# Folding a weight product into an earlier stage of a graph attention kernel, and moving a scaling to ScalarE

## The chip, the cores and the metric

The kernel runs on one core of a Trainium2 chip. The metric is the device time of one execution in microseconds (us). Before the change the median of three runs is 673.04 us (671.46 to 673.52).

## The reference

Two layers run over 4096 nodes of 512 features, with an adjacency matrix of 4096 x 4096 integers in which one entry in about a thousand is set (some four neighbours a node).

```
Wh   = x @ W[h]                                # 8 heads of 64
e    = leaky_relu(f1[i] + f2[j], 0.2)          # f1, f2 = Wh @ a[h] (two halves)
out  = softmax(where(adj > 0, e, -9e15)) @ Wh  # heads side by side
x    = layernorm(x + out)
agg  = (adj > 0) @ x / max(degree, 1)
out  = relu(concat(x @ W_self + b_self, agg @ W_nb + b_nb) @ W_comb + b_comb)
x    = layernorm(x + out)
```

The second layer has no nonlinearity between its two products, so that x @ (W_self W_c1) and agg @ (W_nb W_c2) do, with W_c1 and W_c2 the halves of W_comb. The kernel makes these two 512 x 512 products on the chip; in the code they are m1 (W_self) and m2 (W_nb), and the biases go the same way into one row, brow.

## The kernel before, in words

The nodes are 32 blocks of 128 rows, and the adjacency is used as a list of neighbours a node. The work has three stages. The order of the instructions is written out by hand; each engine carries out its own in that order and waits on semaphores where data or a buffer is missing.

**The lists** (loop over b, from line 929). SP's queue loads x (line 338, 256 KB a block) and adj (line 413, two tiles of 1 MB a block, four buffers named at). ScalarE turns each tile into a mask (mask_adj, line 419), which frees the adj buffer. PE transposes x (line 346; ScalarE copies the result, lines 352 and 359), multiplies it with the weights of the first layer (node_half, line 367; VectorE copies, line 371), and packs the masks into keys (fold_adj, line 437). VectorE takes the largest keys (line 452). Every four blocks a decode (line 454) makes lists, indices and owner tables out of the keys; it is a generator, and each call of some(lists) runs one piece of it, most of them short VectorE work. POOL stores the rows into the table t0 (line 926).

**The joint** (lines 955 to 1013). m2's weights wr and wc are loaded on SP's queue behind adj of block 30, ahead of that of block 31. fold_weights(loaded, place2, "pw") then makes m2 in 16 steps. For each of four chunks, PE transposes a slice of the weights (turned, line 293), ScalarE copies it (line 294), PE does four matmuls (line 305, two instructions each), one a step, and ScalarE copies the sum back into the weights' own tile (line 309). The steps stand between the last masks and folds of blocks 30 and 31. The first two gathers of table rows stand there too; the buffer of the second lies where the adj tiles were, so it waits for the last mask.

**The attention stage** (loop over i from -3 to 33, line 1021). One turn has several blocks in work at different depths. For each block POOL gathers five table rows a node (line 612: three of the node's own list, two from a list that the block shares). VectorE adds and weighs them (lines 645, 662, 670, 686). PE adds the shared rows (a_shared, line 696). VectorE takes the reciprocal of the softmax sum (line 704). The eight heads are then scaled: six on ScalarE, one instruction each (line 712), and two in one VectorE instruction (line 715). VectorE adds x (line 722), ScalarE normalises (root and norm, lines 730 to 739). PE multiplies with m2 to get z (line 744), ScalarE copies it (line 748) and SP stores it in t1 (line 749). PE transposes the block, ScalarE copies it (line 352), and SP stores it in xt (line 752). Five gather buffers stand for the rows. Each turn from i = -2 on also runs one piece of the remaining decodes, and from i = 17 on the pieces of late_lists (line 550). From i = 28 on POOL gathers z rows for the last stage: gather_early(b) reads t1 up to block 25 + b, so it waits until those z are stored.

At i = 7 SP loads W_self into m1 and W_c1 into wc; at i = 16 to 19 VectorE adds the self bias (line 324), and at i = 20 sum_bias (line 329) makes the bias row.

**The last stage** (from line 1072). For each block PE adds the shared z rows (g_shared, line 783) and x @ m1 (g_self, line 776), onto a bias row that ScalarE has copied (line 767). VectorE adds gathered rows (lines 761 and 763) and scales and clips (lines 799 and 803); ScalarE normalises; SP stores. POOL gathers five z rows a node and block, with seven buffers. Between the first two blocks' shared sums and the first x @ m1 stands the fold of W_self, all 16 steps:

```
    for _ in fold_weights(loaded, place, "key"):
        pass
```

Of the kernel before, what the change touches and what calls it, by code (L numbers as in the profile page):

```python
# [31 lines left out]
F32 = mybir.dt.float32  # L32
# [80 lines left out]
def listed_layers(  # L113
# [34 lines left out]
    FIRST = (0, 1, 3)  # L148
    EARLY = NB - 3
    LB = NB - 2  # L150
    HA = 6
# [145 lines left out]
    def fold_weights(loaded, place, bank):  # L297

        wr, wc = loaded
        wT = turned(wr, 0, place(0), bank)  # L300
        for c in range(FB):
            nxt = turned(wr, c + 1, place(c + 1), bank) if c + 1 < FB else None
            mp = ps.tile([P, HD], F32, name="mp")
            for d in range(FB):
                nc.tensor.matmul(  # L305
                    mp, lhsT=wT[:, d, :], rhs=wc[:, d, :], start=(d == 0), stop=(d == FB - 1)
                )
# [398 lines left out]
    def a_scale(b):  # L706

        for h in range(HA):
            a, q = divmod(h, H // 2)
            o = a * HD + (1 - a) * H + q * D  # L710
            s = NM[b][:, o : o + D]
            nc.scalar.mul(s, s, RD[b][:, h : h + 1])  # L712
        o = HD + HH - (H - HA) * D
        s = NM[b][:, o : HD + HH].rearrange("p (h d) -> p h d", d=D)
        nc.vector.tensor_tensor(
            s, s, RD[b][:, HA:].unsqueeze(2).to_broadcast([P, H - HA, D]), OP.mult
        )
# [98 lines left out]
    def some(todo):  # L816
        for p in todo:
            next(p, None)
# [105 lines left out]

    def store(w, row, eng=nc.scalar):
        eng.dma_start(t0[2 + w * P : 2 + (w + 1) * P, :], row[:, 0:TW])

    w, lists = 0, []
    for b in range(LB - 1):
        for k in range(1 + (b in AHEAD)):  # L930
            load_x(w + k + XL)
        load_adj(b + 2, ap)
        if b == 4:
            pads(wp)
# [12 lines left out]
        for k in range(2):  # L947
            some(lists)
        if b == 25:
            pieces = mean_row(w_sb, sums, xa)  # L950
# [4 lines left out]
    m2 = weight(fp, "wr")  # L955
    loaded = load_fold(1, w_nb, m2, weight(fc, "wc"))
# [3 lines left out]
    mask_adj(LB, 0)  # L960
# [6 lines left out]
    def place(c):  # L967
        return wp.tile([P, FW], F32, name="row", bufs=2)[:, 0:FIN]

    def place2(c):  # L970
        return last.rearrange("p (a g) k -> p a (g k)", a=2)[:, c % 2, :]

    def pieces(n, todo):
        for k in range(n):
            next(todo)

    gps = [gather_buffer(0)]
    G0[0] = gather(t0, 0, gps[0])
    mask_adj(LB, 1)
    key_bank(LB + 1)  # L980
    m2s = fold_weights(loaded, place2, "pw")
    pieces(1, m2s)
    fold_adj(LB, dp)
    max_keys(LB)
    pieces(3, m2s)
    mask_adj(LB + 1, 0)
    for k in range(4):
        some(lists)
    pieces(3, m2s)
    mask_adj(LB + 1, 1)  # L990
    pieces(1, m2s)
# [5 lines left out]
    pieces(2, m2s)  # L997
    fold_adj(LB + 1, dp)
    max_keys(LB + 1)
    pieces(2, m2s)  # L1000
# [11 lines left out]
    a_owners(0, wp)  # L1012
# [8 lines left out]
    for i in range(-3, NB + 2):  # L1021
# [76 lines left out]
    for _ in fold_weights(loaded, place, "key"):  # L1098
        pass
# [452 lines left out]
```

## Time and profile before

| what | us |
|---|---|
| median of three runs | 673.04 |
| the profiled execution, its own time | 674.27 |
| its span, first to last instruction | 672.6 |
| busy: PE / VectorE / ScalarE / POOL | 597.7 / 472.4 / 476.6 / 352.6 |
| last adj load issued by SP | 210.7 |
| first gather / second block's first gather on POOL | 220.39 / 230.58 |
| first and last shared sum of the attention stage on PE (block 0, block 31) | 245.15 / 455.88 |
| first shared sum of the last stage | 472.25 |
| matmuls of W_self's fold, from and to | 477.56 / 494.29 |
| last gather issued | 652.2 |
| last shared sum (block 31) | 659.24 |

The page gives busy times for each engine, a strip of 40 slices (17 us each), the chain of work that ended last, the costliest groups of instructions, and the DMA issues. A group's line reads: line of the code, engine, operation, output and input tiles, number, busy time, mean ns of one; then how long the engine stood idle just before and what ended it. PE's matmuls are pipelined, so busy shares say little about their rate; the time from one start to the next says more.

### The profile page before, as it was taken

The page shows a single profiled execution, that of the slowest core. Times are in us where ns is not written, and L with a number is a line of the kernel's source. Part 1 is how long each engine was busy: PE and PEld are TensorE (multiplying, and loading weights), DVE is VectorE, ACT ScalarE, POOL GpSimd, SP SyncE. Part 2 cuts the span into 40 slices and gives each one's busy share as a digit, 9 for nine tenths or more (in the row PEclk, how much of TensorE's full clock was granted, in tenths as well). Part 3 has the DMA queues.
Part 4 walks back from the last instruction along what each step waited for, and adds up shares of the span by engine and source line. Part 5 has one row for each costly group of instructions (what it writes and reads, how often), then busy time and mean ns, then how long its engine had stood idle before and what let it go on. Part 6 is the DMA issues. An engine that isn't in the chain of part 4 may idle for free.

```text
span 672.6 us, 8973 instructions
## 1 busy us (share of the span) xinstructions
PE 597.7 (89%) x2229; PEld 346.2 (51%) x2230; DVE 472.4 (70%) x1293; ACT 476.6 (71%) x1249; POOL 352.6 (52%) x474
## 2 busy tenths in 40 slices
PE   4788989898798958978899889999899999999993
PEld 2566767666665335545455456564444444444441
DVE  6236867868786569999899999992315665666663
ACT  2688888788886326888788778996326677677664
POOL 5111111111112577777777756547777677777760
PEclk9988989989999876999999999999999999999997
DMA  8999999999999577989998987859879898999991
GB/s 247 408 408 407 409 407 408 407 410 408 402 405 405 182 210 229 290 287 298 391 283 299 281 260 224 297 183 295 284 221 307 255 329 310 307 317 308 312 310 67
DMA packets 92037, 209.63 MB, mean 312 GB/s; under 512 B 13694, under 2 KB 13702, under 8 KB 91978
## 3 DMA queue, kind: packets, MB, share of 16 engines
q1 hardware_dynamic: 63024, 114.05, 45.3%
q0 software_dynamic: 28624, 94.39, 43.9%
q10 hardware_dynamic: 330, 0.54, 0.3%
q8 instruction: 20, 0.33, 0.2%
q14 instruction: 39, 0.32, 0.2%
HBM read 175.25 MB, written 33.69 MB: 311 GB/s over the span
## 4 chain that ended last, share of the span: by engine, by line
PE 51%; DMA 26%; DVE 8%; ACT 7%; issue 3%; POOL 3%; SPq 1%; ACTq 0%; DVEq 0%; POOLq 0%
DMA at<-in_adj_dram 15%; PE nm L776 8%; PE pw L776 8%; PE pw L744 8%; DMA g<-t,idx 8%; PE pw L367 6%; PE num L696 5%; PE nm L783 4%; PE pw L783 4%; ACT ab L419 4%; PE tp L305 3%; POOL g L612 3%; DMA wc<-in_L_gnn_W_comb_dram 2%; DVE g L662 2%; PE tp L346 2%
## 5 line engine op out<-in xcount | busy, mean ns | idle before, releaser
L612 POOL DMA_INDIRECT g<-t,idx x290 | 276.1, 952 | 106.9 <-issue 37.5
L419 ACT ACTIVATE ab<-at 128x2048 bf16<-128x2048 int32 x64 | 122.5, 1915 | 32.4 <-DMA at<-in_adj_dram 26.7
L367 PE MATMUL pw<-w_sb,xT 128*128 128x264 f32 x512 | 135.2, 411 | 8.1 <-issue 3.8
L744 PE MATMUL pw<-wr,xT 128*128 128x512 f32 x256 | 116.5, 598 | 3.2 <-ACT xT L352 3.2
L367 PEld LDWEIGHTS pw<-w_sb,xT 128*128 128x128 f32 x512 | 97.2, 199 | 37.0 <-issue 7.2
L374 POOL COPY lst<-row 128x8 f32<-128x8 f32 x32 | 6.5, 203 | 165.0 <-DVE row L371 152.2
L696 PE MATMUL num<-g,own 128*128 128x264 f32 (+1 forms) x256 | 71.7, 429 | 18.7 <-DVE num L686 10.2
L662 DVE TENSOR_TENSOR g<-g,ew 128x1024 f32<-128x1024 f32 x64 | 77.4, 1210 | 0.0
L744 PEld LDWEIGHTS pw<-wr,xT 128*128 128x128 f32 x256 | 48.5, 192 | 52.2 <-issue 46.2
L696 PEld LDWEIGHTS num<-g,own 128*128 128x128 f32 x256 | 51.2, 210 | 32.5 <-DVE num L686 12.8
L712 ACT ACTIVATE num<-num,rd 128x64 f32<-128x64 f32 x192 | 54.7, 285 | 10.0 <-DVE rd L704 4.8
L776 PE MATMUL nm<-m,xT 128*128 128x512 f32 x128 | 57.5, 592 | 0.0
L776 PE MATMUL pw<-m,xT 128*128 128x512 f32 x128 | 57.5, 592 | 0.0
L371 DVE COPY row<-pw 128x264 f32<-128x264 f32 x64 | 27.3, 426 | 33.4 <-PE pw L367 21.4
L799 DVE SCALAR_TENSOR_TENSOR sm<-y,lst,nm 128x512 f32<-128x512 f32 x16 | 12.1, 754 | 52.4 <-PE nm L793 28.7
L346 PEld LDWEIGHTS tp<-ident,xs 128*128 128x128 f32 x256 | 32.2, 148 | 29.5 <-issue 11.5
L686 DVE TENSOR_TENSOR num<-num,g 128x512 f32<-128x512 f32 x64 | 44.7, 699 | 2.2
L346 PE MATMUL tp<-ident,xs 128*128 128x128 f32 x256 | 41.1, 285 | 5.7 <-DVE tl L570 2.5
L776 PEld LDWEIGHTS nm<-m,xT 128*128 128x128 f32 x128 | 24.3, 190 | 30.6 <-issue 30.6
L776 PEld LDWEIGHTS pw<-m,xT 128*128 128x128 f32 x128 | 24.3, 190 | 30.6 <-issue 30.1
L612 POOL DMA_INDIRECT g<-t,idxe x30 | 28.5, 949 | 19.6 <-DVE num L670 9.1
L730 ACT ACTIVATE xs<-y,ln_sum 128x512 f32<-128x512 f32 x32 | 23.3, 728 | 17.1 <-DVE y L722 17.1
(219 smaller groups left out, 981.1 us busy)
## 6 DMA issues: line engine op xcount, KB each, us to landing
at<-in_adj_dram SPq DMA_DIRECT2D x64, 1024.0 KB, 10.7
xt<-xT SPq DMA_DIRECT2D x32, 256.0 KB, 4.3
t<-row SPq DMA_DIRECT2D x32, 256.0 KB, 3.9
xT<-xt SPq DMA_DIRECT2D x32, 256.0 KB, 5.1
out_dram<-row SPq DMA_DIRECT2D x32, 256.0 KB, 5.5
t<-row POOLq DMA_DIRECT2D x31, 260.0 KB, 5.5
xs<-in_x_dram SPq DMA_DIRECT2D x31, 256.0 KB, 10.7
g<-t,idx POOLq DMA_INDIRECT x290, 5.0
```

The source lines that it names most:

```text
L346: nc.tensor.transpose(tp[:, c, :], xs[:, b, ts(c, P)], ident)
L367: nc.tensor.matmul(pw, lhsT=xT[:, c, :], rhs=w_sb[:, c, k * HW : (k + 1) * HW], start=(c == 0), stop=(c == FB - 1),)
L371: nc.vector.tensor_copy(row[:, k * HW : (k + 1) * HW], pw)
L419: nc.scalar.activation(ab, loads.pop((b, h)), AF.Relu, accum_out=asum[:, b, h : h + 1])
L612: nc.gpsimd.indirect_dma_start(out=out, out_offset=None, in_=table, in_offset=bass.IndirectOffsetOnAxis(ap=at, axis=0),)
L662: nc.vector.tensor_tensor(gv, gv, E[b][:, sl].unsqueeze(3).to_broadcast([P, sl.stop - sl.start, H, D]), OP.mult,)
L686: nc.vector.tensor_add(halves_of(NM[b]), halves_of(NM[b]), G0[b][:, k, H:TW].rearrange("p (a c) -> p a c", a=2),)
L696: nc.tensor.matmul(NM[b][:, a * HD : a * HD + r.stop - r.start], lhsT=OWN[b][:, k, :], rhs=G0[b][:, K0 + k, r], start=False, stop=(k == KH ...
L712: nc.scalar.mul(s, s, RD[b][:, h : h + 1])
L744: nc.tensor.matmul(pz, lhsT=xT[:, c, :], rhs=m2[:, c, :], start=(c == 0), stop=(c == FB - 1))
L776: nc.tensor.matmul(NM[b], lhsT=xT[:, c, :], rhs=m1[:, c, :], start=False, stop=(c == FB - 1), skip_group_check=True,)
L783: nc.tensor.matmul(NM[b], lhsT=OWN[b][:, k, :], rhs=g[:, K0 + k, 0:HD], start=False, stop=(k == KH - 1), skip_group_check=True,)
```

## The change

It has four parts.

1. W_self and W_c1 are loaded at b = 1 of the lists. fold_weights makes m1 there in four chunks of four steps, behind blocks 3, 9, 16 and 20. It uses the PSUM banks "pw" for both the transposes and the sums, and slices of the tile last for the transposed weights. The self bias is added at b = 21 to 24. The load at i = 7, the bias steps at i = 16 to 19 and the fold of the last stage are gone; sum_bias moves from i = 20 to i = 8.
2. ScalarE scales all eight heads; the VectorE instruction of line 715 is gone.
3. From i = 0 on a piece of the lists runs in three of four turns, and late_lists is entered at i = 21 instead of 16.
4. m2's weights are loaded ahead of adj of block 30 (at b = 28) instead of behind it. In the joint the steps of m2's fold stand earlier among the masks and folds, and its last four, as well as the first owner copies, stand in turn i = -3.

The diff, cut to its core:

```diff
+    FOLDS = (3, 9, 16, 20)
-    HA = 6
...
-    def fold_weights(loaded, place, bank):
+    def fold_weights(loaded, place, bank, out="mp"):
...
-            mp = ps.tile([P, HD], F32, name="mp")
+            mp = ps.tile([P, HD], F32, name=out)
...
     def a_scale(b):
-        for h in range(HA):
+        for h in range(H):
...
             nc.scalar.mul(s, s, RD[b][:, h : h + 1])
-        o = HD + HH - (H - HA) * D
-        s = NM[b][:, o : HD + HH].rearrange("p (h d) -> p h d", d=D)
-        nc.vector.tensor_tensor(
-            s, s, RD[b][:, HA:].unsqueeze(2).to_broadcast([P, H - HA, D]), OP.mult
-        )
...
     for b in range(LB - 1):
...
+        if b == LB - 2:
+            m2 = weight(fp, "wr")
+            loaded = load_fold(1, w_nb, m2, weight(fc, "wc"))
         load_adj(b + 2, ap)
+        if b == 1:
+            loaded = load_fold(0, w_self, m1, weight(fc, "wc"))
+            m1s = fold_weights(loaded, place, "pw", "pw")
+            biased = fold_bias(loaded, bcol[:, 0:FB])
...
+        if b in FOLDS:
+            steps(4, m1s)
+        if b > FOLDS[-1]:
+            next(biased, None)
...
-    m2 = weight(fp, "wr")
-    loaded = load_fold(1, w_nb, m2, weight(fc, "wc"))
     load_adj(LB + 1, ap)
     row = node_block(w, xT, keep=True)
     key_bank(LB)
-    mask_adj(LB, 0)
     store(w, row)
...
     G0[0] = gather(t0, 0, gps[0])
+    m2s = fold_weights(loaded, place, "pw")
+    steps(1, m2s)
+    mask_adj(LB, 0)
+    steps(3, m2s)
     mask_adj(LB, 1)
     key_bank(LB + 1)
-    m2s = fold_weights(loaded, place2, "pw")
-    pieces(1, m2s)
+    steps(3, m2s)
+    mask_adj(LB + 1, 0)
+    steps(1, m2s)
     fold_adj(LB, dp)
     max_keys(LB)
-    pieces(3, m2s)
-    mask_adj(LB + 1, 0)
     for k in range(4):
         some(lists)
-    pieces(3, m2s)
     mask_adj(LB + 1, 1)
-    pieces(1, m2s)
...
-        if i > -3:
+        if -3 < i < 0 or i % 4 < 3 and i >= 0:
             some(lists)
-        if i == 16:
+        if i == 21:
             lists = [late_lists(dp, last.rearrange("p g (a k) -> p (g a) k", a=2))]
...
-        pieces({-3: 2, -2: 2}.get(i, 0), m2s)
-        if on(i + 4) or i == -3:
+        if i == -3:
+            a_owners(0, wp)
+        if on(i + 4):
             a_owners(i + 4, wp)
+        if i == -3:
+            steps(4, m2s)
...
-        if i == 7:
-            loaded = load_fold(0, w_self, m1, weight(fc, "wc"))
-        if 16 <= i < 20:
-            if i == 16:
-                biased = fold_bias(loaded, bcol[:, 0:FB])
-            next(biased)
-        if i == 20:
+        if i == 8:
             sum_bias()
...
-    for _ in fold_weights(loaded, place, "key"):
-        pass
```

More of the change, by code (lines that the diff above doesn't have):

```diff
@@ L923, in listed_layers, with place, steps @@
     last = oo.tile([P, G, KH * P], F32, name="last")
+    def place(c):
+        return last.rearrange("p (a g) k -> p a (g k)", a=2)[:, c % 2, :]
+    def steps(n, todo):
+        for k in range(n):
+            next(todo)
     def store(w, row, eng=nc.scalar):
@@ L965, in listed_layers @@
     xa_cm.__exit__(None, None, None)
[L967 to L975, printed above, removed]
     gps = [gather_buffer(0)]
     G0[0] = gather(t0, 0, gps[0])
+    m2s = fold_weights(loaded, place, "pw")
+    steps(1, m2s)
+    mask_adj(LB, 0)
+    steps(3, m2s)
     mask_adj(LB, 1)
     key_bank(LB + 1)
-    m2s = fold_weights(loaded, place2, "pw")
-    pieces(1, m2s)
+    steps(3, m2s)
+    mask_adj(LB + 1, 0)
+    steps(1, m2s)
     fold_adj(LB, dp)
     max_keys(LB)
-    pieces(3, m2s)
-    mask_adj(LB + 1, 0)
     for k in range(4):
         some(lists)
-    pieces(3, m2s)
     mask_adj(LB + 1, 1)
-    pieces(1, m2s)
     ap_cm.__exit__(None, None, None)
@@ L996, in listed_layers @@
         some(lists)
-    pieces(2, m2s)
+    steps(2, m2s)
     fold_adj(LB + 1, dp)
     max_keys(LB + 1)
-    pieces(2, m2s)
+    steps(2, m2s)
     bp_cm.__exit__(None, None, None)
@@ L1011, in listed_layers @@
     G0[2] = gather(t0, 2, gps[2])
-    a_owners(0, wp)
     lists = [chain(lists[0], decode(NB - G, dp, on_last))]
```

## The prediction

> **What bounds the kernel now.** I read the page's slices first, then the chain that ended last, then each stage's windows, and last the timelines of the queue that the windows left under suspicion. The slices (17 us each):
>
> ```profile
> DMA  8999999999999577989998987859879898999991
> GB/s 247 408 408 407 409 407 408 407 410 408 402 405 405 182 210 229 290 287 298 391 283 299 281 260 224 297 183 295 284 221 307 255 329 310 307 317 308 312 310 67
> ```
>
> Up to about 221 us (the lists) the transfers run flat out at 405 to 410 GB/s: bytes set that stage. PE is close behind, 167.19 us busy of the 190 from 10 to 200. The attention stage and the last stage do not saturate the transfers. Where the fold of W_self stands, the chain shows PE:
>
> ```profile
> 477.73 3.45 PE tp L305 x8
> ...
> 481.84 3.71 PE tp L305 x8
> ...
> 486.21 3.71 PE tp L305 x8
> ...
> 490.59 3.70 PE tp L305 x8
> ```
>
> From 475.79 to 494.13, 18.3 us, PE does only this fold, and everything behind it waits. Read alone, that says 18 us can go. But a second queue runs beside PE to the end. The timeline of POOL, where every gather of a list slot is one instruction:
>
> ```profile
> 447.18 0.95 POOL L612 DMA_INDIRECT g<-t,idxe  x1 [0.30 <-issue]
> 450.11 0.94 POOL L612 DMA_INDIRECT g<-t,idxe  x1 [1.98 <-DVE num L686]
> 451.36 0.95 POOL L612 DMA_INDIRECT g<-t,idxe  x1 [0.30 <-DVE y L722]
> ```
>
> A gather starts every 1.2535 us (451.36 - 450.11 and so on; it lasts 0.95 and 0.30 lie between), five to a block, 6.27 us a block. The one at 450.11 is the first of early block 1; after it come 160 more (24 + 6 late + 26 x 5), the last at 652.2 by the trace, only 1.5 us later than 450.11 + 160 x 1.2535 = 650.7. So **POOL is full from 450 us to the end**, while PE needs 5.15 us a block there. PE's last block starts at 659.24, some 3 us after its rows have landed: the fold gave the gathers their lead, and without it they set the end. I call the start of that run T1 (450.11).
>
> What sets T1 is the attention stage: early block 1 reads z of block 26, whose store is issued at about 445.2 and lands up to 4.7 us later. The windows of that stage (us, then busy time of PE, weight loads, DVE, ACT, POOL, then clock, DMA share, GB/s):
>
> ```profile
> 258.00:330.00 72.00, 62.65 (x210) 37.46 (x209) 69.49 (x170) 57.10 (x185) 53.72 (x57) 0.95 0.92 300
> 330.00:400.00 70.00, 60.49 (x211) 35.86 (x210) 66.29 (x152) 57.57 (x182) 51.14 (x55) 0.98 0.90 290
> 400.00:465.00 65.00, 64.05 (x220) 38.72 (x221) 56.23 (x127) 57.75 (x182) 38.17 (x41) 0.97 0.77 246
> ```
>
> To 400 DVE is full (95 to 97%) and after it PE (99%). In turns of the loop: PE's shared sums of block 1 start at 252.69, those of block 27 at 432.75, 26 turns of 6.93 us. A turn with a max piece of the lists (0.85 us) took 6.47, so DVE's own work is 5.62 a turn; without pieces PE's 5.80 (3.43 + 0.51 + 1.86) shows. ScalarE in such a 5.80 turn:
>
> ```profile
> 438.25 0.20 ACT L652 ACTIVATE ew<-e 128x40 f32<-128x40 f32 x1
> ...
> 442.29 1.87 ACT L712 ACTIVATE num<-num,rd 128x64 f32<-128x64 f32 x6
> 444.08 0.20 ACT L652 ACTIVATE ew<-e 128x40 f32<-128x40 f32 x1
> ```
>
> From 438.25 to 444.08 its instructions follow each other without a gap: 5.83, so it is as full as PE, though the window says 89%. Six scalings take 1.79, 0.30 each.
>
> **The change, part by part.**
>
> *Weights of W_self, moved to block 1 of the lists.* 2 x 1.05 MB on SP's queue behind adj of block 3 and ahead of x and adj of block 4, in a stage bound by bytes: 2.10 MB / 407 GB/s = 5.15 us later for all that follows. The last adj bytes land near 221.2 now (the rate falls there), 226.4 after. In the attention stage the same bytes go (SP at 310.4 and 310.9), where 310 to 330 show a share of 1.0; I take 0 for that, at most 1.5 us of gathers that land sooner. The z weights move ahead of adj 30 on the same queue: same bytes, those of adj 30 land 5.15 us later, and wc is there by 226.4 - 4 x 2.57 = 216 instead of 218.
>
> *Fold of W_self in four chunks.* Each is eight L305 matmuls (3.45) and four transposes (0.6), 4.1 us of PE; the first has four more and must wait for ScalarE's copies of them, which stand behind the mask of block 4 (42.4 to 46.95 now), so 6.5. Sum 18.8. Its cover is PE's waiting for masks and rows from block 3 on: 2.22, 0.74, 1.99, 1.76, 1.14, 1.17, 0.85, 1.64, 2.02 = 13.5 us. Such a wait costs more than its length:
>
> ```profile
> 94.04 0.87 PE L437 MATMUL nm<-ab,fold 128*32 128x512 bf16 x6 [1.99 <-ACT ab L419]
> ```
>
> and the window behind it (busy of PE, weight loads, DVE, ACT, POOL, then granted clock, DMA share, GB/s):
>
> ```profile
> 94.00:96.00 2.00, 1.96 (x9) 1.06 (x9) 1.06 (x5) 1.56 (x10) 0.00 (x0) 0.56 1.04 413
> ```
>
> After the 1.99 us wait the granted clock is 0.56 and eight L367 matmuls take 3.43 instead of 1.9; four such places hold 4.4 us that a filled wait saves. So PE reaches the end of the lists between 5.3 (18.8 - 13.5, nothing saved) and 0.9 us late against the shifted adj. Chunk by chunk the shift of 5.15 absorbs part of it; I take 1.3. [...] ScalarE's eight copies (0.48 each) and DVE's four bias steps (0.67 each, blocks 21 to 24) fall into stages where these engines are 81% and 70% busy: 0, up to 1 us.
>
> *The joint of the stages.* Let P0 be the end of fold_adj of block 29 on PE: 214.1 now, 214.1 + 5.15 + 1.3 = 220.6 after. The new order puts on ScalarE behind P0: two turnings and copies (1.6), a mask (1.9), a wait for four matmul pairs (1.1), copy 0.5, mask 1.9, key 0.5, copy 0.5, mask 1.9, copy 0.5, mask 1.9, 0.3 to POOL: 12.6. Gather 1 needs the last mask (its buffer lies where adj lay): 220.6 + 12.6 = **233.2, against 230.58 now, 2.6 later**. The last adj (226.4) is there in time. Gather 0 waits for the store of row 31, some 6 us behind P0, and ends just before. Of this order POOL, then every block, waits.
>
> *ScalarE scales all heads.* DVE loses L715 (0.20 from start to start), ScalarE gains two scalings: 5.80 + 0.60 = 6.40 a turn. DVE's turn is 5.62 - 0.20 = 5.42 plus its piece; DVE's sums wait for the scale, and with 5.42 in 6.40 they are early enough. PE's 5.80 and the gathers' 6.27 fit under it. So 25 turns of 6.40 = 160.0; above that come turns with a large piece: blocks' steps 2, 4, 5 with bias 0.6 each, the bias sum at 8 0.8, the degree piece 0.55, the piece with PE's transposed table 0.9, others 2.0: 5.9. The first turn waits for its gather, 7.4 as now. Sum 173.3 instead of 180.06: 6.8 less. Skipping every fourth turn costs nothing, since the pieces end at step 21 and gather 28 needs them at 22. The spread late pieces cost 0.35 to 0.8 each, in the sum; now they and the self bias made turns of 8.95, 8.98 and 8.65. Moving the first owner copies and four fold steps in step -3 costs 0: PE waits there for gathers.
>
> [...]
>
> *The last stage without the fold.* PE is freed of 18.3 us, and the gathers set the end. T1 after: block 1 at 252.69 + 2.6 = 255.3, block 27 at + 173.3 = 428.6, then the 17.36 us that now lie between block 27 and T1, + 1.1 for the slower turns, + 0.6 because four more early blocks wait for z at 6.40 instead of 6.27: **447.7**. From T1: 160 gathers 200.6, the last one's own 0.95, landing 4.0 (rows: 3.7 to 5.0), second half of the shared sum 1.0, moments 1.5, and from the last Square (663.91) to the end 8.7: 216.75. Span 664.4, 8.2 less than 672.6. Of that 5.7 come with T1 unmoved (450.1 + 216.75 = 666.9) and 2.4 from T1. The profiled execution took 674.27 for its span of 672.6, the median of three runs is 673.04; I take the difference off the median: **664.8 us**.
>
> **Rivals.**
> - *The fold's full time goes* (PE sets the end): 673.04 - 18.3 = 654.7. For it speaks the chain; against it POOL without a gap after 450.
> - *The turn falls to the gathers' pace*: 26 x 6.27 = 163 instead of 173.3, T1 10 us sooner, 655. For it: DVE's relief; against: ScalarE's gapless row.
> - *The attention stage gains nothing*, ScalarE's 0.60 meeting DVE's pieces: 26 x 6.93, T1 6.8 later, 671.6: no measurable change.
> - *Slower: the chunks delay the joint.* PE's work in the lists is not hidden, since each chunk's copies stand behind masks on ScalarE, and the adj buffers come free late. Nothing hidden: P0 = 214.1 + 5.15 + 18.8 = 238.1, 17.5 later than I take, 682. It decides from 8.2 us of lag beyond mine, P0 past 228.8. Against it: 13.5 us of waits.
>
> **Chances.** The forecast, with 660 to 669 as its own range: 0.58. The full fold 0.05, the gathers' pace 0.10, no gain in the attention stage 0.17, delay at the joint 0.10. A measurement of this kernel tells 0.3% (2 us) from no change. Faster: 0.58 (less 0.02 that may end near 671), 0.05, 0.10 and 0.05 of the no-gain case, 0.76; same 0.14; slower 0.10. The range, 656 to 673, takes in the turn from 6.27 to 6.93 and PE's lag from 0.9 to 5.3, and leaves out the slow rival and the full fold.
>
> **What would show it.** Right: adj ends near 226 with 400 GB/s to there; gather 1 near 233; turns of 6.4 to 6.9 with ScalarE gapless; the POOL run starts near 448 and has no gap; in the last ten blocks PE waits for gathers. Wrong: the rate sags in the lists; turns near 6.3 or 6.9; PE gapless to the end while POOL waits.

## The result, and the profile after

The change makes the kernel slower: 679.41 us (median of 20 runs, 674.76 to 683.95) against 671.49 us for the kernel before beside it (20 runs), a ratio of 1.0101 with a 95 % interval of 1.008 to 1.0122 (6.8 us by the ratio; the medians are 7.9 apart). The forecast was 664.8 us, with a range to 673. What came is the rival "the chunks delay the joint", which the prediction had given a chance of 0.10.

The profiled execution of the kernel after has a span of 679.1 us (its own time 680.92), against 672.6 before. Four marks divide the difference of 6.5:

| mark (us) | before | after | forecast |
|---|---|---|---|
| P0, fold_adj of block 29 done on PE | 214.1 | 230.5 | 220.6 |
| shared sum of block 1 | 252.69 | 266.70 | 255.3 |
| 26 turns from there (block 1 to 27) | 180.06 | 175.07 | 173.3 |
| T1, first gather of early block 1 | 450.11 | 460.43 | 447.7 |
| T1 to the end of the span | 222.49 | 218.67 | 216.75 |

The attention stage is 5.0 us shorter and the last stage 3.8, nearly as forecast; block 1 starts 14.0 us late, where 2.6 was forecast. So the loss lies in the lists. The slices of the page (17 us each) show it:

```profile
DMA  8998999999998967899998999938989899999982
GB/s 240 407 406 317 391 407 408 410 407 408 409 336 315 403 186 216 249 290 291 276 297 284 307 288 291 299 132 265 314 265 312 297 309 319 313 304 318 298 279 86
```

Before, the rate held 402 to 410 GB/s from the second slice to the thirteenth. Now it sags twice: to 317 in the fourth slice (behind the first chunk), and to 336 and 315 in the twelfth and thirteenth. Finer windows of the kernel after (us, then busy time of PE, weight loads, VectorE, ScalarE, POOL, then clock, DMA share, GB/s):

```profile
60.00:65.00 5.00, 5.00 (x32) 3.69 (x31) 1.85 (x7) 4.63 (x13) 0.03 (x1) 1.00 0.54 209
65.00:70.00 5.00, 5.00 (x31) 3.59 (x30) 4.72 (x21) 5.00 (x7) 1.32 (x4) 1.00 0.84 302
70.00:75.00 5.00, 5.00 (x31) 3.69 (x30) 3.96 (x20) 5.00 (x14) 1.45 (x8) 1.00 1.00 342
...
195.00:200.00 5.00, 2.31 (x12) 1.51 (x5) 4.00 (x13) 3.11 (x4) 0.00 (x0) 0.77 0.74 245
200.00:205.00 5.00, 5.00 (x28) 3.64 (x27) 3.19 (x11) 2.93 (x10) 1.34 (x4) 0.89 0.93 307
205.00:210.00 5.00, 5.00 (x31) 3.68 (x30) 4.66 (x25) 5.00 (x7) 0.94 (x4) 1.00 0.57 209
210.00:215.00 5.00, 5.00 (x27) 3.12 (x25) 4.74 (x18) 3.67 (x7) 0.94 (x4) 1.00 1.03 329
```

At 407 GB/s the first sag loses some 4.5 us of transfers and the second some 6.6. The first comes from the timeline of ScalarE (start, duration, operation, idle time before and what ended it):

```profile
48.53 1.91 ACT L419 ACTIVATE ab<-at 128x2048 bf16<-128x2048 int32 x1 [6.19 <-DMA at<-in_adj_dram]
...
51.79 1.91 ACT L419 ACTIVATE ab<-at 128x2048 bf16<-128x2048 int32 x1 [1.26 <-DMA at<-in_adj_dram]
...
53.70 1.05 ACT L294 COPY last<-pw 128x512 f32<-128x512 f32 x2
```

and from that of PE:

```profile
54.32 5.38 PE L305 MATMUL pw<-wc,last 128*128 128x512 f32 x8 [7.78 <-ACT last L294]
```

The load of the weights makes adj of block 4 late, so ScalarE's masks wait 6.19 and 1.26 us for it. The copies of the first chunk's transposed weights are written behind these masks, and PE, which has the chunk next, stands idle for 7.78 us, with the rows of the next blocks behind it. The forecast had some 1.8 us of wait there (its 6.5 for the first chunk, less 4.1 of work and 0.6 for the further transposes).

The second sag lies in blocks 22 to 24. PE first, then VectorE:

```profile
186.74 3.25 PE L367 MATMUL pw<-w_sb,xT 128*128 128x264 f32 x8 [2.32 <-DVE sums L356]
...
198.09 3.51 PE L367 MATMUL pw<-w_sb,xT 128*128 128x264 f32 x8 [2.69 <-DVE sums L356]
```

```profile
194.85 0.75 DVE L324 SCALAR_TENSOR_TENSOR brow<-wc,bcol,brow 128x512 f32<-128x512 f32 x1
...
197.35 0.69 DVE L356 TENSOR_REDUCE sums<-pw 128x4 f32<-128x512 f32 x1
```

A bias step of 0.75 us, all four of them put at 0 to 1 us together, stands in VectorE's order ahead of the row sum that PE waits for. PE waits 2.32 and 2.69 us, and its next eight matmuls take 3.25 and 3.51 instead of 1.95. The lists before had one such wait near their end (2.02).

What followed the joint came nearly as forecast. The turns in the windows of the attention stage:

```profile
258.00:330.00 72.00, 58.26 (x181) 35.04 (x182) 67.50 (x151) 58.64 (x193) 54.63 (x58) 0.88 0.86 265
330.00:400.00 70.00, 66.56 (x230) 39.04 (x229) 61.39 (x139) 64.09 (x208) 52.94 (x57) 0.98 0.92 291
400.00:465.00 65.00, 60.66 (x214) 34.95 (x214) 61.30 (x137) 61.05 (x199) 38.53 (x41) 1.00 0.77 245
```

VectorE falls from 66.29 to 61.39 us in the middle window and ScalarE rises from 57.57 to 64.09. ScalarE in a turn without a gap:

```profile
419.93 2.52 ACT L712 ACTIVATE num<-num,rd 128x64 f32<-128x64 f32 x8
422.37 0.20 ACT L652 ACTIVATE ew<-e 128x40 f32<-128x40 f32 x1
...
426.42 2.52 ACT L712 ACTIVATE num<-num,rd 128x64 f32<-128x64 f32 x8
```

426.42 - 419.93 = 6.49, where the forecast had 6.40. And POOL, whose gathers then run on with only 0.77 and 0.59 us of further waits:

```profile
460.43 0.95 POOL L612 DMA_INDIRECT g<-t,idxe  x1 [1.90 <-DVE num L686]
461.68 0.96 POOL L612 DMA_INDIRECT g<-t,idxe  x1 [0.31 <-DVE kxl L587]
```

At the end PE waits for them, as forecast:

```profile
659.86 1.96 PE L778 MATMUL nm<-g,own 128*128 128x512 f32 x4 [0.80 <-DMA g<-t,idx]
665.73 3.43 PE L778 MATMUL pw<-g,own 128*128 128x512 f32 x4 [3.92 <-DMA g<-t,idx]
```

### The profile page after: what moved, and what is told of

Its sections match the earlier page's. It is cut to its first block, busy times and chain, and to the rows that moved or that the text cites. A ratio compares the mean times of both kernels' runs of the same rounds, so it can differ in the third digit from the quotient of the medians.

```text
span 679.1 us, 8998 instructions
## 1 busy us (share of the span) xinstructions
PE 599.0 (88%) x2229; PEld 342.6 (50%) x2230; DVE 466.2 (69%) x1261; ACT 493.3 (73%) x1313; POOL 353.0 (52%) x474
## 5 line engine op out<-in xcount | busy, mean ns | idle before, releaser
L367 PE MATMUL pw<-w_sb,xT 128*128 128x264 f32 x512 | 133.6, 407 | 9.8 <-DVE sums L356 5.8
L739 PE MATMUL pw<-wr,xT 128*128 128x512 f32 x256 | 117.9, 604 | 4.6 <-ACT xT L352 4.6
L367 PEld LDWEIGHTS pw<-w_sb,xT 128*128 128x128 f32 x512 | 96.3, 198 | 38.2 <-issue 8.9
L696 PE MATMUL num<-g,own 128*128 128x264 f32 (+1 forms) x256 | 70.2, 422 | 14.8 <-DVE num L686 6.9
L712 ACT ACTIVATE num<-num,rd 128x64 f32<-128x64 f32 x256 | 73.3, 286 | 12.3 <-DVE rd L704 5.0
L346 PEld LDWEIGHTS tp<-ident,xs 128*128 128x128 f32 x256 | 32.2, 147 | 27.5 <-issue 13.6
L778 PE MATMUL pw<-g,own 128*128 128x512 f32 x64 | 32.1, 624 | 6.3 <-DMA g<-t,idx 6.3
```

Of the source, the lines that this page charges most:

```text
L346: nc.tensor.transpose(tp[:, c, :], xs[:, b, ts(c, P)], ident)
L367: nc.tensor.matmul(pw, lhsT=xT[:, c, :], rhs=w_sb[:, c, k * HW : (k + 1) * HW], start=(c == 0), stop=(c == FB - 1),)
L696: nc.tensor.matmul(NM[b][:, a * HD : a * HD + r.stop - r.start], lhsT=OWN[b][:, k, :], rhs=G0[b][:, K0 + k, r], start=False, stop=(k == KH ...
L739: nc.tensor.matmul(pz, lhsT=xT[:, c, :], rhs=m2[:, c, :], start=(c == 0), stop=(c == FB - 1))
L778: nc.tensor.matmul(NM[b], lhsT=OWN[b][:, k, :], rhs=g[:, K0 + k, 0:HD], start=False, stop=(k == KH - 1), skip_group_check=True,)
```

## The experiments

The theory: work on PE in the lists is not hidden; the adj buffers come free late and the joint with them. The rival: the bytes and the new order of the joint cost, not the chunks' work. Further questions came up on the way: what made the turns shorter, and where the fold belongs. Ratios are against the kernel before run beside each kernel. In the table, gather 0 is the first on POOL.

| run | us | ratio, 95 % | P0 | gather 0 | 26 turns | T1 | T1 to end |
|---|---|---|---|---|---|---|---|
| before | 670.43 to 672.61 | 1 | 214.1 | 220.39 | 180.06 | 450.11 | 222.49 |
| after | 679.41 | 1.0101, 1.008 to 1.0122 | 230.5 | 237.96 | 175.07 | 460.43 | 218.67 |
| e1 bias at 17 to 20 | 676.58 | 1.0065, 1.0042 to 1.0088 | 225.7 | 233.18 | 174.53 | 454.51 | 218.09 |
| e2 load 5, chunk 9 | 682.04 | 1.0146, 1.0108 to 1.0185 | 230.6 | 238.17 | 174.66 | 459.35 | 218.35 |
| e3 both moves | 680.99 | 1.0129, 1.0092 to 1.0166 | 229.5 | 237.00 | 174.32 | 458.29 | 219.31 |
| e4 before, no fold | 668.6 | 0.9948, 0.9922 to 0.9974 | 216.5 | 222.72 | 178.21 | 446.18 | 217.92 |
| e5 after, no chunks | 669.46 | 0.9982, 0.996 to 1.0004 | 220.7 | 226.85 | 174.62 | 448.34 | 219.06 |
| e6 after, no W_self in lists | 663.35 | 0.9877, 0.9846 to 0.9908 | 213.9 | 220.17 | 174.61 | 442.09 | 219.51 |
| e7 after, six heads | 675.13 | 1.0054, 1.0029 to 1.008 | 227.2 | 234.65 | 170.88 | 452.85 | 219.05 |
| e8 before, fold in turns | 673.43 | 1.0038, 1.0008 to 1.0067 | 215.5 | 221.68 | 184.97 | 451.47 | 216.63 |
| e9 fold last, rest kept | 672.16 | 1.0013, 0.9981 to 1.0045 | 214.7 | 220.93 | 179.43 | 448.02 | 223.88 |
| e10 before, all ScalarE | 679.07 | 1.0115, 1.0068 to 1.0163 | 214.1 | 220.41 | 179.85 | 450.19 | 224.91 |
| e11 a step a block | 682.76 | 1.0175, 1.0127 to 1.0223 | 232.5 | 238.79 | 174.55 | 460.80 | 217.70 |
| e12 e6 with six heads | 661.04 | 0.9847, 0.9797 to 0.9896 | 216.0 | 222.18 | 171.32 | 441.28 | 218.22 |

The marks come from one profiled execution each. The lists of e7 are those of the kernel after and yet its P0 is 3.3 us earlier; before, e4, e8 and e10 share their lists too, and their P0 lies between 214.1 and 216.5. The 26 turns of the six runs that have the attention stage of the kernel after (after, e1, e2, e3, e5, e11) agree within 0.8 us, but before and e4, one code up to the last stage, differ by 1.9 us in the 26 turns and by 3.9 at T1. So single marks are good to some 2 to 4 us.

**e1: the bias steps moved.**

```diff
-        if b > FOLDS[-1]:
-            next(biased, None)
+        if 16 < b <= 20:
+            next(biased)
```

> The changed kernel with the four self-bias steps on VectorE at blocks 17 to 20 instead of 21 to 24. Theory (three places in the lists make the joint late; one is VectorE at blocks 22 to 24, where the bias step of 0.67 us stands ahead of the row sum that frees PE's bank, so PE waits 2.3 and 2.7 us, runs 1.4 us slower behind each wait, and adj falls to 245, 307 and 209 GB/s from 195 to 210 us, some 6.6 us of transfer lost): about 5 us come back, 674 to 676, no sag after 190 us, gather 0 near 233 instead of 238. Rival (PE's 18.8 us of added work make the lists long wherever they stand): within 1.5 us of the changed kernel.

Gather 0 came 4.8 us earlier and the second sag shrank (353, 331 and 361 GB/s from 195 to 210). The time fell by 0.0036 of 671.5 = 2.4 us, half of what was expected, and the two intervals touch. Later steps of the kernel gave some back. The steps do cost; that they cost all of the second sag isn't shown.

**e2, e3: the load at b = 5, the first chunk behind block 9** (e3 with the bias of e1).

```diff
-    FOLDS = (3, 9, 16, 20)
+    FOLDS = (9, 12, 16, 20)
...
-        if b == 1:
+        if b == 5:
```

> The changed kernel with W_self loaded at block 5 and the chunks behind blocks 9, 12, 16 and 20. Theory (the first chunk behind block 3 waits 7.8 us on PE for ScalarE's copies behind the mask of block 4, whose adj is late by the load just ahead of it, and adj falls to 209 and 302 GB/s from 60 to 70 us, 4.4 us lost): no 7.8 us wait, no sag at 60 to 70, about 4 us come back, 675 to 677. Rival (the lag only moves, since PE's work is the same): within 1.5 us of the changed kernel, with a sag at a later block.

> Both moves together. Theory: the two losses are separate, 4.4 + 6.6 us of transfer come back, gather 0 near 227, T1 near 450, 668 to 670, faster than before (671.5). Rival (PE's work is what makes the lists long): 677 or more.

The wait of 7.78 us and the sag at 60 to 70 are gone, and nothing is gained: the rate sags at 100 to 165 us instead (to 342, 344 and 309 GB/s in windows of 5 us; in e3 to 208), and P0 is where it was. So the stall that the eye falls on first was not decisive. The theory in its first form (the order of waits behind the first chunk) fell here; what stood was that the chunks cost as much in this place. The first chunk of e2 waits only 0.94 us for its copies, but PE's waits for masks up to P0 are 10.3 us, where the kernel after has 4.9.

**e4: the kernel before without its fold of W_self.**

```diff
-    for _ in fold_weights(loaded, place, "key"):
-        pass
```

> The kernel before with the fold of W_self left out of the last stage (x is multiplied with W_self itself; nothing else changes). Theory (the gathers on POOL set the end once PE has no fold): T1 stays at 450, PE waits for gathers in the last blocks, the time falls by 4 to 6 us only, 665.5 to 667.5. Rival (the fold's 18.3 us are on the path): 653.

Of the 18.3 us that the chain shows for the fold, some 4 can be had (668.6 against 672.61 us; by the ratio 0.9948 it is 3.5, with an interval of 1.7 to 5.2). PE then waits for gathers up to its last block:

```profile
650.34 3.75 PE L783 MATMUL pw<-g,own 128*128 128x512 f32 x4 [3.84 <-DMA g<-t,idx]
```

This was the forecast's own account of the last stage, and it holds.

**e5: the kernel after without the chunk steps.**

```diff
-        if b in FOLDS:
-            steps(4, m1s)
```

> Built on the kernel after. The eight chunk steps of the fold in the lists are taken out; the load of W_self's weights and the bias steps stay where they are. Left out: the product W_self W_c1, so x is multiplied with W_self itself. Theory (the chunks' work and waits on PE, not the bytes, make the joint late): only the 5.15 us of bytes are left, gather 0 near 225.5 instead of 237.96, T1 near 448, 666 to 668 us. Rival (the bytes and the joint's new order are what costs): gather 0 past 232, 675 us or more.

The theory: P0 at 220.7 and gather 0 at 226.85, with 0.9982 instead of 1.0101, some 8 us; the time is 1.5 us over the theory's range. The chunks are the larger part of the cost. The whole lists, from 10 us to P0, in one window each (same columns as above): before,

```profile
10.00:214.10 204.10, 181.29 (x1018) 130.60 (x1018) 141.90 (x512) 163.34 (x357) 36.05 (x128) 0.96 1.05 406
```

without chunks (e5),

```profile
10.00:220.70 210.70, 182.27 (x1019) 131.31 (x1020) 144.24 (x516) 161.35 (x355) 36.28 (x128) 0.95 1.04 403
```

and after:

```profile
10.00:230.40 220.40, 195.90 (x1067) 138.12 (x1067) 144.38 (x516) 164.27 (x363) 36.24 (x128) 0.95 1.01 385
```

PE's time outside its work is 204.1 - 181.3 = 22.8 us before, 28.4 in e5, 24.5 after. The chunks add 13.6 us of busy time to e5, and 9.7 us come out at P0 (6.5 by the P0 of e7, whose lists are the same); only 3.9 went into waits. Which waits went and which came is told by the view of waits (who waited, for whom: us in total, times, longest), from 10 us to P0. Without chunks (e5),

```profile
PE key L437 <- ACT ab L419: 11.4, 5, 4.2
PE nm L437 <- ACT ab L419: 8.5, 6, 2.1
...
ACT xT L359 <- PE tp L346: 4.0, 5, 1.7
...
PE pw L367 <- DVE sums L356: 3.0, 2, 2.7
```

and after:

```profile
ACT xT L359 <- PE tp L346: 11.7, 6, 4.0
PE pw L305 <- ACT last L294: 7.8, 1, 7.8
ACT m L309 <- PE pw L305: 7.5, 4, 5.0
PE pw L367 <- DVE sums L356: 5.8, 3, 2.7
...
PE key L437 <- ACT ab L419: 4.3, 2, 2.7
...
PE nm L437 <- ACT ab L419: 0.6, 1, 0.6
```

The chunks did fill waits for masks: 19.9 us of them became 4.9, all ahead of the first chunk, and between 55 and 179 us PE waits only 1.9 us in all, against 9.3 before and 8.8 in e5. But other waits came: PE's 7.8 us for the first chunk's own copies and 5.8 for VectorE's row sums, and ScalarE's for PE (11.7 instead of 4.0 for the transposes of x, 7.5 for the chunks' sums). In all PE's waits from block 3 on are 15.5 us after, where the kernel before had 13.5.

**e6: no load, chunks or bias of W_self in the lists.**

```diff
-        if b == 1:
-            loaded = load_fold(0, w_self, m1, weight(fc, "wc"))
...
-        if b in FOLDS:
-            steps(4, m1s)
-        if b > FOLDS[-1]:
-            next(biased, None)
...
+        if i == 7:
+            nc.sync.dma_start(m1, w_self.rearrange("(c p) o -> p c o", p=P))
```

> Built on the kernel after. Load, chunks and bias steps of W_self are all taken out of the lists; W_self comes unfolded in turn 7 of the attention stage. Left out: the product W_self W_c1 and the bias folded with W_self. What stays of the change: the joint's new order, ScalarE scaling all heads, the spread pieces. Theory: the joint is some 4 us earlier than in the kernel before (gather 0 near 220, gather 1 near 226.7 instead of 230.58), 26 turns in 173 to 175, T1 near 443, 659 to 662 us. Rival (the new order and scaling give nothing without room in the lists): T1 near 450, 668 us, as the kernel before without its fold.

As the theory said, 1.4 us above its range: gather 1 at 226.96 instead of 230.58, T1 at 442.09. So the joint's new order gives 3.6 us of gather 1 in this pair of executions. Over the runs at 671 us it is less: gather 1 comes at 228.56 to 230.58 in the old order (before, e4, e8, e10) and at 226.96 to 229.03 in the new one (e6, e9, e12), 1.7 us apart on the mean. Load and bias cost 0.0105 of 671.5, or 7 us (e5 against e6), chunks 8.

**e7: six heads on ScalarE again, in the kernel after.**

```diff
+    HA = 6
...
-        for h in range(H):
+        for h in range(HA):
...
+        nc.vector.tensor_tensor(
+            s, s, RD[b][:, HA:].unsqueeze(2).to_broadcast([P, H - HA, D]), OP.mult
+        )
```

> Built on the kernel after, the whole computation. ScalarE scales six heads and VectorE the last two again, as before the change. Theory (the shorter turns come from this move): 26 turns back to 178 to 180 us and a time 3 to 5 us over the kernel after's, near 683 us. Rival (the shorter turns come from the pieces that left the stage, fold and self bias): 26 turns within 1 us of 175.07, the same time as the kernel after.

Both were wrong, the theory in sign: the 26 turns fell to 170.88, and the time to 1.0054. ScalarE in a turn that carries no piece:

```profile
392.76 1.87 ACT L713 ACTIVATE num<-num,rd 128x64 f32<-128x64 f32 x6
...
398.60 1.87 ACT L713 ACTIVATE num<-num,rd 128x64 f32<-128x64 f32 x6
```

398.60 - 392.76 = 5.84 against 6.49 in the kernel after. The turns got shorter because of what had left them: the self bias, the load and, in one turn of four, the piece (what each of the three gives isn't separated). The move of the scaling costs 4 us of that. Handing that work from VectorE to ScalarE doesn't pay here: in the kernel before, in a turn of 5.80 us without a piece, VectorE's own work comes to 5.62 (6.47 of a turn with a piece, less 0.85 for it), and ScalarE had no gap from 438.25 to 444.08.

**e8: the kernel before, its fold spread over turns 10 to 25, a step a turn.**

```diff
+        if i == 9:
+            m1s = fold_weights(loaded, place3, "pw")
+        if 10 <= i < 26:
+            pieces(1, m1s)
...
-    for _ in fold_weights(loaded, place, "key"):
-        pass
```

> Built on the kernel before, the whole computation. The fold of W_self is taken out of the last stage and spread instead over turns 10 to 25 of the attention stage, one step a turn; the lists and the joint are left alone. Theory (PE has 0.6 to 1 us of slack in a turn that VectorE sets): T1 at most 2 us later, the last stage set by the gathers, 666 to 670 us. Rival (PE becomes the bound of these turns, 5.80 + 0.86 + 0.15 = 6.8 us with the slower clock on top): T1 later by 4 us or more, 671 us or more.

The rival, in the turns and the time: 26 turns in 184.97, 4.9 us more than before. Eleven of them took 6.48 to 6.49, PE's 5.80 with a step on top. Four of these stand where turns of 5.63 to 5.80 had been, and lost 3.0 us. The longest turn, 10.52 instead of 6.62, has the first step, whose two sets of transposes wait for their copies; in it ScalarE also waits 1.26 and 0.64 us for stores issued behind the load of the weights. So not all of the loss is PE as the bound. The last stage came down to 216.63 from T1, the gathers' pace; what it gave the turns took, and the time is 1.0038. T1 is only 1.4 us later, since block 1 came 3.1 us earlier in this execution.

**e9: the joint's order and the spread pieces kept; load, bias, fold and six heads as before.**

```diff
+        if i == 7:
+            loaded = load_fold(0, w_self, m1, weight(fc, "wc"))
+        if 16 <= i < 20:
...
+    for _ in fold_weights(loaded, row_place, "key"):
+        pass
```

> The whole computation. Kept from the change: the joint's new order and the spread pieces. Put back as in the kernel before: W_self loaded in turn 7, its bias in turns 16 to 19, its fold in the last stage, six heads on ScalarE and two on VectorE. Theory (the joint's order and the spread pieces give, the fold in the lists and the all-ScalarE scaling take): gather 0 near 220, gather 1 near 227, 26 turns in 172 to 175, T1 near 442, the first shared sum of the last stage near 463 instead of 472.25, 661 to 665 us, below the kernel before by 1 per cent or more. Rival (the order and the pieces give only what the fold's leaving frees): 26 turns of 178 or more, T1 past 447, 669 to 672 us.

Gather 1 came at 227.93, as the theory said, and the gain was lost in the turns: one took 12.96 us (323.57 to 336.53). ScalarE and VectorE in it:

```profile
327.13 0.59 ACT L748 COPY row<-pw 128x512 f32<-128x512 f32 x1 [3.47 <-DMA t<-row]
328.85 0.59 ACT L352 COPY xT<-tp 128x512 f32<-128x512 f32 x1 [1.14 <-DMA xt<-xT]
```

```profile
333.79 0.30 DVE L715 TENSOR_TENSOR num<-num,rd 128x128 f32<-128x128 f32 x1 [4.47 <-ACT num L712]
```

ScalarE waits for the store of a z row before it may write the row's buffer again, and then for the store of a block in xt. SP had issued the 2.1 MB of weights at 305.85 and 306.44, and these two stores right behind, at 310.83 and 311.31. The first holds ScalarE until 327.13, and the second landed 17.2 us after its issue, where the median of such stores is 4.6. The same store took 14.3 us in the kernel before, where it held up ScalarE for 0.84 us. No row shows when the two stores began; that they stood behind the 2.1 MB issued just ahead of them on the same queue is the author's guess. e12, whose load in turn 7 is half as large, fits it: there ScalarE waits for no store, and the same turn took 5.80. That the order in the queue is the cause was not tested at the usual 671 us.

**e10: the kernel before with all heads on ScalarE.**

```diff
-        for h in range(HA):
+        for h in range(H):
...
-        nc.vector.tensor_tensor(
...
```

> The kernel before with one edit: ScalarE scales all eight heads, VectorE none. The whole computation. Theory (ScalarE, gapless already, becomes the bound, and VectorE's sums wait for it): the 26 turns get longer, 183 to 186 us instead of 180.06, and the time 674 to 678 us. Rival (the forecast's view: turns of 6.40 set by ScalarE, VectorE relieved): 26 turns in 173 to 176, 666 to 668 us.

The 26 turns are the same (179.85): turns with a piece gain 0.2, those without lose 0.68. The time is 1.0115. The profiled execution was the fastest of six (676.81) and shows 2.0 us of the loss, in a later start of the last stage (474.22 against 472.25, the four turns behind block 27 being 2.4 us longer); where the rest goes isn't known. Neither theory has it right, but the move alone certainly doesn't help.

**e11: one fold step to a block, behind blocks 4 to 19, bias as in e1.**

```diff
-        if b in FOLDS:
-            steps(4, m1s)
-        if b > FOLDS[-1]:
-            next(biased, None)
+        if 4 <= b < 20:
+            steps(1, m1s)
+        if 16 < b <= 20:
+            next(biased)
```

> Built on the kernel after, the whole computation. The sixteen fold steps go one to a block, behind blocks 4 to 19, instead of four at a time; the bias steps stand behind blocks 17 to 20. Theory (the bursts of 4 us and their copies are what PE can't make up): gather 0 near 229 to 231 instead of 233.18 in the run with the bias steps moved alone, no sag of the rate under 380 GB/s before 180 us, 672 to 674 us. Rival (PE has no room in the lists however the work is cut): gather 0 at 233 or later, 676 us or more.

The rival, and worse than it: P0 at 232.5 and 1.0175. The rate sags all through blocks 4 to 19:

```profile
GB/s 252 400 406 408 385 330 407 364 355 390 373 392 339 407 233 213 254 291 291 279 286 290 297 292 288 294 144 268 309 278 305 293 313 302 316 318 309 305 286 97
```

So smaller steps don't help. That the work as such doesn't fit isn't shown by it, since another wait came with the smaller steps: a chunk's sum now holds one of the two PSUM banks pw over four blocks, and PE waits for VectorE's copies out of them,

```profile
PE pw L367 <- DVE row L371: 7.0, 8, 1.6
```

7.0 us in eight waits, where the kernel before has one of 2.2.

**e12: e6 with six heads on ScalarE.** The edits are those of e6 and e7 together.

> As the run without W_self's load, chunks and bias in the lists, with six heads on ScalarE and two on VectorE. Left out: the product W_self W_c1 and the bias folded with W_self. Theory (the all-ScalarE scaling costs 4 us in 26 turns): 26 turns in 170 to 171 instead of 174.61, T1 near 438, 658 to 660 us. Rival (the scaling's place matters only beside the fold in the lists): 26 turns near 174.6, 663 us.

171.32 for the 26 turns against 174.61 in e6, 0.9847 against 0.9877: nearly as the theory said (the time is 1 us over its range, T1 3 us), and the turns of e7 once more. The times' intervals overlap, so it is the turns that carry this.

**e13 to e18: load in parts, bias late, half of the fold in turns.** These six ran where the kernel before itself took 785.68 and 786.33 us.

```diff
-        if i == 7:
-            loaded = load_fold(0, w_self, m1, weight(fc, "wc"))
+        if i == 6:
+            loaded = (m1, weight(fc, "wc"))
+        if 6 <= i < 6 + 2 * FB:
+            load_part(0, w_self, *loaded, i - 6)
```

e13 and e17 have this edit on e9, e16 on the kernel before. e14 also moves the bias from turns 16 to 19 to turns 28 to 31. e15 and e18 have both, and

```diff
+        if i == 13:
+            m1s = fold_weights(loaded, turn_place, "pw")
+        if i in (14, 16, 17, 18, 20, 21, 22, 24):
+            steps(1, m1s)
```

> The run with the fold in the last stage and the rest of the change kept, with one edit: the two loads of 1.05 MB for W_self are cut into eight of 0.26 MB, one in each of turns 6 to 13. The whole computation. Theory (the 2.1 MB in one piece hold up the store of a z row, and through its row buffer ScalarE and every engine): no turn over 9.5 us, 26 turns in 172 to 175 instead of 179.43, first shared sum of the last stage near 466, 665 to 667 us. Rival (the same bytes cost the same in parts): 26 turns near 179, 671 to 673 us.

> The run with the load in eight parts, and W_self's bias steps moved from turns 16 to 19 to turns 28 to 31, where VectorE has run out of pieces of the lists. The whole computation. Theory (a bias step of 0.74 lengthens a turn that VectorE sets): 26 turns 2 to 3 us shorter than in the run with the parts alone, 662 to 665 us. Rival (the steps only move their 0.7 us each to the tail, behind which T1 lies as well): first shared sum of the last stage and time within 1 us of that run.

> The run with the load in parts and the bias late, and half of the fold (eight of its sixteen steps) spread over eight turns that also carry a piece of the lists; the other half stays in the last stage. The whole computation. Theory (with the joint and the turns earlier PE's fold sets the end by some 5 us, and a turn that VectorE sets has 0.6 to 1 us of room on PE): T1 at most 1 us later, PE's last stage 9 us shorter, the gathers set the end, 658 to 662 us. Rival (PE bounds the turns): 26 turns 4 us longer, no better than the run without this edit.

> The kernel before with one edit: the two loads of 1.05 MB for W_self are cut into eight of 0.26 MB, one in each of turns 6 to 13. The whole computation. Theory (in the kernel before the load holds up ScalarE once, 2.31 and 0.84 us near 330 us): 26 turns 1 to 3 us shorter, 668 to 670 us. Rival (nothing waits long for it): the time of the kernel before within 0.3 per cent.

> The run with the load of W_self in eight parts (turns 6 to 13), fold in the last stage, bias in turns 16 to 19, joint's order and spread pieces kept; once more, beside a kernel before at its usual 671 us. The whole computation. Theory (the 2.1 MB in one piece hold up the store of a z row): no turn over 9.5 us, 26 turns in 172 to 175 instead of 179.43, first shared sum of the last stage near 466, 665 to 667 us. Rival (the same bytes cost the same in parts): 26 turns near 179, 671 to 673 us.

> The run with the load in parts, the bias steps in turns 28 to 31 and half of the fold in eight turns that carry a piece; once more, beside a kernel before at its usual 671 us. The whole computation. Theory: bias late saves 2 us of the 26 turns, eight fold steps cost at most 1 us there, PE's last stage is 9 us shorter, the gathers set the end, 658 to 662 us. Rival (PE bounds the turns, as where all sixteen steps went into turns: 26 turns 184.97): 26 turns past 177, 668 us or more.

None of these numbers could be met there. The lists are untouched (gather 0 at 220.48 to 222.32), but from then on ScalarE's copies into the z rows wait in several turns for something that the profile calls remote, as in the timeline of ScalarE in e17:

```profile
435.51 0.59 ACT L755 COPY row<-pw 128x512 f32<-128x512 f32 x1 [4.95 <-remote]
```

and the 26 turns take 200 to 216 us. Why the program is slower there the runs don't tell. Beside their kernel before, e13, e14, e16 and e17 are the same (0.9995, 0.9991, 1.0007 and 1.0017). e15 and e18, which are one kernel, are faster, 0.9909 (0.9875 to 0.9943) and 0.9917 (0.9875 to 0.9958). That kernel was not run at the usual 671 us; why it gains stays open, as does what the load in parts is worth at 671 us.

## Why the prediction was wrong

**The step that failed: the cover of the chunks.** "Its cover is PE's waiting for masks and rows from block 3 on: ... = 13.5 us", with up to 4.4 us of slow clock to be saved, and so "I take 1.3" for PE's lag. Measured: 9.7 us at P0 (e5 against after; 6.5 by the P0 of e7) and 8.0 us in the time; P0 at 230.5, past the 228.8 that the prediction had named as the point from which its slower rival decides (227.2 in e7, whose lists are the same). The waits were added up as if any chunk could use any of them and no new ones would come. Those between 55 and 179 us were used, 9.3 us before and 1.9 after. But PE now waits 7.8 us for the first chunk's copies and 5.8 for VectorE's row sums, so that from block 3 on 15.5 us of waits stand where 13.5 were to be filled. A wait of PE is the end of a chain through other engines (load, mask on ScalarE, copy or sum on VectorE), and the work that is new to PE made those engines late too: ScalarE waits 11.7 us for the transposes of x, where it waits 4.0 without chunks. PE's time outside its work was 22 to 28 us in every version of the lists. Three placements of the chunks (after and e1, e2 and e3, e11) all cost, each with other waits; that no placement could do better isn't shown.

**The slow clock, 4.4 us to be saved.** Nothing of it shows at P0. e10 has the lists of the kernel before. Behind a wait of 2.13 us at the same place its clock stayed at 1.00 (94 to 96 us), and the eight matmuls took 2.05:

```profile
94.03 0.61 PE L437 MATMUL nm<-ab,fold 128*32 128x512 bf16 x6 [2.13 <-ACT ab L419]
94.56 2.05 PE L367 MATMUL pw<-w_sb,xT 128*128 128x264 f32 x8
```

PE's work in these lists is 177.1 us instead of 181.3, and P0 is the same 214.1. So the slow places didn't set P0 before the change. Nor does the length of a wait alone decide whether the clock falls: behind 2.13 us it was 1.00 here, behind 1.99 us in the kernel before it was 0.56.

**Bytes.** 5.15 us were forecast, and P0 in e5 is 6.6 us late, 7 us in time with the bias steps. Nearly right. With load and bias alone P0 is at 220.7, where the forecast had it at 220.6 with the chunks.

**First chunk.** Its wait was priced at some 1.8 us and took 7.78: the load in front makes ScalarE's masks late, a link that wasn't followed. It wasn't decisive: without that wait (e2) P0 is the same.

**Bias steps and copies at 0 to 1.** Probably too low: moving the bias steps alone gave 2.4 us back (e1), though its interval overlaps that of the kernel after, and the same move between e2 and e3 gave 0.0017, within the noise.

**The joint.** Gather 1 at P0 + 12.6 was forecast; it came at P0 + 13.9 after, + 13.0 in e5 and in e6. Right within 1.3.

**The attention stage: right number, wrong reason.** 173.3 forecast, 175.07 measured, and the turn of ScalarE is 6.49 as against 6.40. But the prediction gave the 6.8 us to the scaling, as DVE's relief. e7 and e12 show the opposite: with six heads the same stage takes 171, and the scaling takes back 3 to 4 of the 9 us that the moved pieces, bias and load give. So the number fits by luck. That turns without a piece would run at 5.80 with the old scaling stood in its own rows, and wasn't worked out.

**The bytes in the attention stage at 0, at most 1.5.** In the kernel before the rows show 0.84 us of wait for a store issued behind the load, within that. In e9 the turn with two such waits took 12.96 us, some 6 more than the others; if the load is the cause, what the term is worth depends on the turns around it.

**The last stage.** T1 to the end 216.75 forecast, 218.67 after, 216.63 to 219.51 in the eleven versions without the fold there. Right: POOL's gathers set the end, and e4 puts the worth of the fold's place at 3.5 to 4.0 us where the chain shows 18.3. The first rival (the fold's full time goes) is refuted by it.

The bill, from ratios times 671.5 us: what is left of the change without its part in the lists (e6) wins 8.3; load and bias there cost 7.1 (e5 against e6), the chunks 8.0 (after against e5); the sum is the 6.8 measured. Within the 8.3 the traces give the joint 3.7 (block 1 at 248.98 instead of 252.69), the turns 5.4 (8.7 from what left them, less 3.3 for the scaling), and the last stage 3.0, less 1.1 between block 27 and T1. These 11.0 are more than 8.3 because the profiled execution before was 2.8 us above its median. With single marks the division is rough: taken over the runs of either order, block 1 is only 1.4 us earlier on the mean.

No version here beats the kernel before with the whole computation at the usual 671 us: e9 equals it, e7, e8 and the rest are slower.

## What to carry over

The waits of PE, 88 % busy in the lists of the kernel before (167.19 us of 190), were not a sum that new work could draw on: those in the middle of the stage were filled, and as many came elsewhere, for the new work's own inputs and for engines that it had made late. Before moving work, take it out (e4) and look at what the time does: the chain's 18.3 us were worth some 4 where they stood, because a second queue beside PE was full. And when an edit bundles a gain and a loss in one stage, work out the stage with each edit alone; the sum can come out right and the reasons wrong.

## What the runs showed of the hardware

In the kernel after, behind waits of 2.32 and 2.69 us, PE's next eight L367 matmuls took 3.25 and 3.51 us instead of 1.95; the granted clock in the window with the longer one (195 to 200 us) was 0.77. It isn't so each time: in e7, the same lists, the waits were 2.32 and 2.69 us as well, and the eight matmuls took 2.05 behind both:

```profile
186.64 2.05 PE L368 MATMUL pw<-w_sb,xT 128*128 128x264 f32 x8 [2.32 <-DVE sums L357]
...
196.31 2.05 PE L368 MATMUL pw<-w_sb,xT 128*128 128x264 f32 x8 [2.69 <-DVE sums L357]
```

In e9 a 256 KB store issued on SP's queue 4.9 us behind a 1.05 MB load landed 17.2 us after its issue, against a median of 4.6. POOL's indirect gathers start 1.25 us apart in e17 as well (600.07, 601.32), where the 26 turns took 205.68 us. In the kernel before, eight L744 matmuls that start at 434.61 are followed by the next line's at 438.04, 0.43 us for each, while the record of one lasts 592 ns: the records overlap.
